# An adaLN transformer block on one core: out-projection ahead of the scores, down products in groups on alternate rows, the last layernorm in two parts

## Chip, core and metric

The kernel runs on 1 core of one Trainium2 chip. The metric is the device time of one execution in microseconds. Shown runs are compared by their medians.

## The reference

The kernel computes one block of a transformer for a batch of 2 sequences of 1024 rows and 256 columns, all in fp32. Cut to what matters:

```python
mod = (silu(c) @ wmod).reshape(B, 6, 1, 256)
sa, ca, ga, sb, cb, gb = ...                    # ga, gb: kept away from zero
h = layernorm(x) * (1 + ca) + sa
q, k, v = h @ Wq + bq, h @ Wk + bk, h @ Wv + bv # 16 heads of 128
q, k = rotary(q * 128 ** -0.5), rotary(k)
attn = softmax(causal(q @ k.T))                 # per head, 1024 x 1024
x = x + ga * ((attn @ v) @ Wo + bo)
h = layernorm(x) * (1 + cb) + sb
gate, up = qlinear(h, wq_gate, s_gate), qlinear(h, wq_up, s_up)   # 704 hidden units
x = x + gb * qlinear(silu(gate) * up, wq_down, s_down)
```

`qlinear` takes integer weights, less 128, times a scale for each output.

## The kernel before

**Units and slots.** The work of attention is cut into 32 units, one for each sequence and head (`units`, n from 0 to 31; two heads h form a group g that shares its loaded weights). A unit has 8 slots, one for each tile of 128 query rows. The order of all instructions is written out by hand (`tc.manual_schedule()`), so each engine's queue holds its instructions in the order of the program. The engines only wait for one another by semaphores.

**A slot.** In slot i, `score` (L410) multiplies 128 rows of q with the (i+1) x 128 keys that the causal mask leaves, into a tile of `ps_sc` (two buffers), and DVE finds the negative maximum of each row with one masked reduction (L425). `turned` (L452) transposes the exponentials of the slot before on DVE, in 32x32 blocks, into `t32` (L456). After every fourth slot, 16 transfers on SP's queue (L468) move these blocks into `pT`, which completes the transposition. `expo` (L437) makes the exponentials on ACT. Then `project_out` (L502) follows: one matmul `py` (L509) into the only buffer of `ps_y`, and a DVE instruction (L512) that scales by the row's softmax denominator and adds to x. It works on heads of earlier units: in slots 0 to 3 on the rows 512 to 1023 of unit n-2, in slots 4 to 7 on the rows 0 to 511 of unit n-1. After it `release` (L405) runs the part of the rotary product that had been put off, on DVE and POOL. Then come projections of the next unit's q, k (L379) and v (L361), in slots 5 and 6 the product of the previous unit's `pT` with v for its rows 512 to 1023 (`values`, L483, matmul `po`), and in slot 7 the same for the unit's own rows 0 to 511. `extras` spreads further work over the units, among it the layernorm of the second sequence for attention (units 10 to 14) and that of the first sequence for the gated part (units 26 to 30); both put instructions on DVE.

**The gated part.** The hidden layer has 704 units, that is `NF` = 6 chunks: five of 128 and a last one of 64 (`FULL` = 640). `hidden(b, blk, c)` (L525) computes gate and up of one chunk for 512 rows: 4 matmuls of 512 columns, silu on ACT and one product on DVE into `gTs`. The last chunk has gate and up in one matmul pair. In unit 31, slots 1 to 6 hold `hidden(0, 0, c)` with banks from `ps_a`, with `late=False`; the later ones use `ps_sc`. ACT needs one table for exponentials, one for silu and one for the root, and loads it anew at each change. `down(b, blk, j)` (L555) multiplies one tile of 128 rows with the six chunks of `wdT`, adds x on DVE (`yo`) and sends the tile to `out` on SP's queue. `bank` (L496) hands out four PSUM banks in turn: `ps_y`, `ps_o` and twice `ps_a`. The chunk 5 of `wdT` holds its 64 rows twice, in the partitions 0 to 63 and 64 to 127; before, only the first copy is read.

**The end.** After unit 31 come `hidden(0, 1, c)`, the rest of `project_out` and `values`, and the layernorm of the second sequence: `ln_stats` of 8 tiles, one `ln_sqrt` (ACT), `ln_scale` and `ln_turn` (transposes on PE, `ptx`, and a DVE instruction L217) for two blocks of four tiles. Between them stand `down(0, 0, j)`. Then `hidden(1, 0, c)` and `hidden(1, 1, c)` follow, with one `down` of the block before after each of the chunks 1 to 4, and four `down` at the very end.

Of the kernel before, what the change touches and what calls it, by code (L numbers as in the profile page):

```python
# [11 lines left out]
F32 = mybir.dt.float32  # L12
I32 = mybir.dt.int32
AF = mybir.ActivationFunctionType
ALU = mybir.AluOpType
PSUM = bass.MemoryType.PSUM

P = 128
B, S, D = 2, 1024, 256
H, DH = 16, 128  # L20
HID = 704
NT = S // P
# [15 lines left out]
def adaln_block(ctx: ExitStack, tc: tile.TileContext, a, cos_d, sin_d, out):  # L38
# [457 lines left out]
    def bank(name):  # L496

        pool, tag = banks[turn[0] % 4]
        turn[0] += 1
        return pool.tile([P, 512], F32, tag=tag, name=name)  # L500

    def project_out(u, t, late=False):  # L502

        b, g, h = u
        if t % 4 == 0:
            nc.vector.reciprocal(rdens[u][:, t : t + 4], dens[u][:, t : t + 4])
        name = f"py_{b}{g}{h}{t}"
        py = bank(name) if late else ps_y.tile([P, 512], F32, tag="y", name=name)
        nc.tensor.matmul(  # L509
            py[:, :D], outs[u][:, ts(t, P)], weights[b, g]["o"][:, h, :], start=True, stop=True  # L510
        )
        nc.vector.scalar_tensor_tensor(  # L512
            x[b][:, t, :], py[:, :D], rdens[u][:, t : t + 1], x[b][:, t, :], ALU.mult, ALU.add
        )
# [10 lines left out]
    def hidden(b, blk, c, late=True):  # L525
        if c == 0:
            gTs[b, blk] = fpool.tile([P, NF, QB], F32, tag="f", name=f"gT_{b}{blk}")
        last = c == NF - 1
        if late:
            pg = ps_sc.tile([P, S], F32, tag="sc", name=f"pgu_{b}{blk}{c}")  # L530
            pgs = [pg[:, ts(j, QB)] for j in range(2)]
        else:
            pgs = [
                ps_a.tile([P, 512], F32, tag="a", name=f"pgu_{b}{blk}{c}{j}") for j in range(2 - last)
            ]
        for pg, n in zip(pgs, ("gate",) if last else ("gate", "up")):
            for k in range(KC):
                nc.tensor.matmul(  # L538
                    pg,
                    wT["last"][:, k, :] if last else wT[n][:, k, ts(c, P)],  # L540
                    h2s[b, blk][:, k, :],
                    start=(k == 0),
                    stop=(k == KC - 1),
                )
        sg = ppool.tile([P, QB], F32, tag="p", name=f"sg_{b}{blk}{c}")
        if last:

            m = HID - FULL
            nc.scalar.activation(sg[m:], pgs[0][:m], AF.Silu)
            nc.vector.tensor_tensor(gTs[b, blk][:m, c, :], sg[m:], pgs[0][m:], ALU.mult)  # L550
        else:
            nc.scalar.activation(sg, pgs[0], AF.Silu)
            nc.vector.tensor_tensor(gTs[b, blk][:, c, :], sg, pgs[1], ALU.mult)

    def down(b, blk, j):  # L555
        t = blk * 4 + j
        pd = bank(f"pd_{b}{t}")
        for c in range(NF):
            m = min(P, HID - c * P)
            nc.tensor.matmul(  # L560
                pd[:, :D],
                gTs[b, blk][:m, c, ts(j, P)],
                wdT[b][:m, c, :],
                start=(c == 0),
                stop=(c == NF - 1),
            )
        yo = rot.tile([P, D], F32, tag="r1", name=f"yo_{b}{t}")
        nc.vector.tensor_tensor(yo, pd[:, :D], x[b][:, t, :], ALU.add)
        nc.sync.dma_start(out[b, ts(t, P), :], yo)


    units = [(b, g, h) for b in range(B) for g in range(NG) for h in range(HG)]
# [53 lines left out]
    with tc.manual_schedule():  # L626
        nc.scalar.activation(
            sc.rearrange("p b k -> p (b k)"), sc.rearrange("p b k -> p (b k)"), AF.Silu
        )
        nc.scalar.activation(warm, eps_t, AF.Sqrt)  # L630
        weights[0, 0] = {}
        load_w(0, 0, "q")
        load_w(0, 0, "k")
        for t, t_d in ((cos_t, cos_d), (sin_t, sin_d)):
            nc.sync.dma_start(t[:, :QB], t_d[:, :QB])
        load_w(0, 0, "v")
        for t in (4, 6):
            load_x(0, t, 2, nc.sync)
        for t, t_d in ((cos_t, cos_d), (sin_t, sin_d)):
            nc.sync.dma_start(t[:, QB:], t_d[:, QB:])  # L640
        nc.sync.dma_start(wga, a["w_gates"])
        nc.sync.dma_start(wmod[:, 1], a["L0_wmod"][1])
        load_proj(*units[2][:2])
        load_out(0, 0)
        nc.gpsimd.memset(bvacc, 0.0)

        for blk, t in enumerate(t32):
            for j in range(3):
                nc.gpsimd.memset(t[:, :, j, 4 * blk + j + 1 :, :], 0.0)
        for t in (0, 2):  # L650
            for j in range(2):
                ln_stats(0, "a", t + j)
            ln_sqrt(0, "a", t, t + 2)
            if t:
                ln_scale(0, "a", 0, (0, 1))
        modulation(0, ps_y, "y")
        ln_scale(0, "a", 0, (2, 3))
        shift_scale(0)
        ln_turn(0, "a", 0, 0, new_hT(0, 0), split=True)
        for t in range(4, NT):  # L660
            ln_stats(0, "a", t)
        ln_sqrt(0, "a", 4, NT)
        for s in ("q", "k"):
            project_qk(units[0], s, 0)
        for t in (0, 2):
            project_v(0, 0, t, *((ps_o, "o"), (ps_y, "y"))[t // 2])
        ln_scale(0, "a", 1)
        release()
        ln_turn(0, "a", 1, 0, new_hT(0, 1), split=True)
        gates()  # L670
        for s in ("q", "k"):
            project_qk(units[0], s, 1)
        nc.gpsimd.dma_start(bo_bc, a["L0_attn_bo"].to_broadcast([P, D]))

        for n, u in enumerate(units):
            b, g, h = u
            prev = units[n - 1] if n else None
            nxt = units[n + 1] if n + 1 < N else None
            nb, ng = (b, g + 1) if g + 1 < NG else (b + 1, 0)
            more = nb < B  # L680
            for i in range(NT):
                ps, nmax = score(u, i)
                if i >= 1:
                    turned(u, i - 1)
                elif prev:
                    turned(prev, NT - 1)
                expo(u, i, ps, nmax)

                if i < 4 and n > 1:
                    project_out(units[n - 2], 4 + i)  # L690
                if i >= 4 and prev:
                    project_out(prev, i - 4)
                release()
                if i in (1, 3, 4, 6) and nxt:
                    project_qk(nxt, *{1: ("q", 0), 3: ("k", 0), 4: ("q", 1), 6: ("k", 1)}[i])
                if i in (5, 6) and prev:
                    values(prev, 1, 4 * (i - 5), 4 * (i - 4))

                if i == 7 and prev:
                    values(u, 0, 0, 4)  # L700
                if n == 1 and i == 1:
                    values(prev, 0, 0, 4)
                if i in (0, 2):
                    if h == 0:
                        project_v(b, g, 4 + i)
                    elif more:
                        project_v(nb, ng, i)
                if not nxt and 1 <= i < 7:
                    hidden(0, 0, i - 1, late=False)
                extras(n, i)  # L710
                if i == 7 and h == 1:
                    if more:
                        load_out(nb, ng)
                    if n + 3 < N:
                        load_proj(*units[n + 3][:2])

        u, prev = units[-1], units[-2]
        turned(u, 7)
        for c in range(4):
            hidden(0, 1, c)  # L720
            project_out(prev, 4 + c, late=True)
            project_out(u, c, late=True)
        values(u, 1, 0, 8)
        hidden(0, 1, 4)
        for t in range(4, NT):
            project_out(u, t, late=True)
        hidden(0, 1, 5)
        for t in range(NT):
            ln_stats(1, "b", t)
        ln_sqrt(1, "b", 0, NT)  # L730
        down(0, 0, 0)
        ln_scale(1, "b", 0)
        down(0, 0, 1)
        down(0, 0, 2)
        ln_turn(1, "b", 0, 2, new_h2(1, 0))
        down(0, 0, 3)
        ln_scale(1, "b", 1)
        for c in range(NF):
            hidden(1, 0, c)
            if c == 0:  # L740
                ln_turn(1, "b", 1, 2, new_h2(1, 1))
            if c in (1, 2, 3, 4):
                down(0, 1, c - 1)
        for c in range(NF):
            hidden(1, 1, c)
            if c in (1, 2, 3, 4):
                down(1, 0, c - 1)
        for j in range(4):
            down(1, 1, j)


def _rotary_tables():
# [65 lines left out]
```

## Time and profile before

| | |
|---|---|
| time, median of 3 runs | 1099.24 us (1099.04 to 1101.0) |
| profiled execution: its own time | 1098.96 us |
| profiled execution: span | 1097.2 us |
| busy PE, DVE, ACT, POOL | 1085.3, 641.6, 508.4, 397.4 us |
| instructions | 12347 |

The profile comes from one execution; its span runs from the first to the last instruction that it shows, and lies 1.76 us under that execution's own time. PE is TensorE's matmuls, PEld its weight loads, DVE is VectorE, ACT ScalarE, POOL GpSimd, SP the SyncE, whose queue issues most transfers. A row of a timeline has the start, the duration, engine and line, the operation, the written and the read tiles and their shapes, how many instructions are merged in it, and in brackets how long the engine had stood idle before it and for whom. In a row of the waits, the engine and line that waited stand first, then for whom, then the time in total, the number of waits and the longest. Durations of matmuls include their filling and draining, which overlaps with the next one's; what one costs in a row of many is seen from start to start.

### The profile page before, as it was taken

Reading aid. Unit: us, or ns where it says so; the run is one execution under the profiler, and the core shown is the slowest. Engines: PE = TensorE matmul, PEld = TensorE weight load, DVE = VectorE, ACT = ScalarE, POOL = GpSimd, SP = SyncE. Lnnn points to the kernel's source line nnn. Section 1 sums busy time; section 2 is a strip of 40 time slices with the busy share of each in tenths; the row PEclk is TensorE's granted clock in tenths of the full one; section 3 lists DMA queues with packets and bytes.
Section 4 is the critical chain, followed back from the end, with each engine's and each line's share of the span. In section 5 each row is a group of like instructions: output and inputs, shape, how many; then the busy total and the mean of one; then the engine's idle time right before and its main releaser. Section 6 shows DMA issues by size and latency. Waiting matters only on the chain.

```text
span 1097.2 us, 12347 instructions
## 1 busy us (share of the span) xinstructions
PE 1085.3 (99%) x3524; PEld 641.0 (58%) x3524; DVE 641.6 (58%) x1418; ACT 508.4 (46%) x953; POOL 397.4 (36%) x364
## 2 busy tenths in 40 slices
PE   9999999999999999999999999999999999999998
PEld 5555555656565565655565666565655556455555
DVE  5556565666766855655566565556668656544311
ACT  5644444544555444444454454444445445641110
POOL 4635353535343343754333533333333334100000
PEclk9999999999999999999999999999999999999999
DMA  6365656657564556465554646464545656431000
GB/s 216 81 146 125 158 127 162 151 115 179 127 147 106 133 120 156 97 148 116 139 130 109 145 109 145 108 147 99 138 97 134 133 124 136 91 83 25 25 20 29
DMA packets 67192, 130.97 MB, mean 119 GB/s; under 512 B 18963, under 2 KB 23315, under 8 KB 67125
## 3 DMA queue, kind: packets, MB, share of 16 engines
q1 hardware_dynamic: 64772, 125.91, 48.6%
q10 hardware_dynamic: 2304, 4.16, 1.2%
q8 instruction: 28, 0.46, 0.2%
q14 instruction: 40, 0.32, 0.1%
q0 software_dynamic: 48, 0.13, 0.1%
HBM read 25.26 MB, written 2.10 MB: 25 GB/s over the span
## 4 chain that ended last, share of the span: by engine, by line
PE 96%; DVE 3%; issue 0%; ACT 0%; POOL 0%; DVEq 0%; ACTq 0%; POOLq 0%
PE ps L422 22%; PE po L483 22%; PE py L509 10%; PE pq L379 10%; PE pk L379 10%; PE pv L361 9%; PE pgu L538 7%; PE pd L560 4%; DVE t L456 1%; DVE ps L425 1%; PE warm_ps L82 1%; DVE x L512 0%; DVE kT L395 0%; PE pm L119 0%; PE pg L150 0%
## 5 line engine op out<-in xcount | busy, mean ns | idle before, releaser
L425 DVE CUSTOM_DVE_ANT_0 ps<-ps,mask 128x128 f32<-128x128 f32 (+7 forms) x256 | 195.6, 764 | 328.6 <-PE ps L422 328.2
L442 ACT ACTIVATE p<-ps,nmax 128x128 f32<-128x128 f32 (+7 forms) x256 | 189.8, 741 | 340.4 <-DVE nmax L425 336.9
L422 PE MATMUL ps<-kT,qT 128*128 128x512 f32 (+3 forms) x768 | 289.6, 486 | 0.7 <-ACT p L442 0.7
L483 PE MATMUL po<-pT,v 128*128 128x512 f32 (+3 forms) x768 | 263.4, 486 | 0.0
L422 PEld LDWEIGHTS ps<-kT,qT 128*128 128x128 f32 x768 | 141.1, 190 | 127.3 <-issue 121.0
L483 PEld LDWEIGHTS po<-pT,v 128*128 128x128 f32 x768 | 145.8, 190 | 115.6 <-issue 92.0
L456 DVE STREAM_TRANSPOSE t<-p 128x128 f32<-128x128 f32 (+7 forms) x256 | 198.2, 774 | 0.3
L509 PE MATMUL py<-wo,o 128*128 128x256 f32 x512 | 156.9, 390 | 5.0 <-DVE x L512 5.0
L392 POOL TENSOR_TENSOR r_k<-r_k,sin_t 128x512 f32<-128x512 f32 x64 | 81.3, 1271 | 208.5 <-ACT r_k L391 208.4
L398 POOL TENSOR_TENSOR kT<-kT,r_k 128x512 f32<-128x512 f32 x64 | 81.5, 1273 | 158.2 <-DVE kT L395 153.0
L392 POOL TENSOR_TENSOR r_q<-r_q,sin_t 128x512 f32<-128x512 f32 x64 | 81.8, 1278 | 148.9 <-ACT r_q L391 145.8
L509 PEld LDWEIGHTS py<-wo,o 128*128 128x128 f32 x512 | 90.0, 190 | 64.9 <-issue 30.1
L361 PE MATMUL pv<-wv,hT 128*128 128x256 f32 x512 | 120.9, 379 | 1.1 <-DVE qT L395 1.1
L379 PE MATMUL pq<-hT,wq 128*128 128x512 f32 x256 | 120.5, 593 | 0.5 <-DVE hT L217 0.5
L512 DVE SCALAR_TENSOR_TENSOR x<-py,rden,x 128x256 f32<-128x256 f32 x256 | 116.0, 455 | 7.5 <-PE py L509 0.7
L379 PE MATMUL pk<-hT,wk 128*128 128x512 f32 x256 | 120.3, 592 | 0.0
L391 ACT ACTIVATE r_q<-pq,cols 64x512 f32<-64x512 f32 x128 | 87.5, 683 | 47.9 <-PE pq L379 47.0
L361 PEld LDWEIGHTS pv<-wv,hT 128*128 128x128 f32 x512 | 97.1, 190 | 15.2 <-DVE qT L395 1.2
L391 ACT ACTIVATE r_k<-pk,cols 64x512 f32<-64x512 f32 x128 | 87.4, 683 | 18.0 <-PE pk L379 15.9
L398 POOL TENSOR_TENSOR qT<-qT,r_q 128x512 f32<-128x512 f32 x64 | 83.6, 1306 | 25.5 <-DVE qT L395 23.1
L379 PEld LDWEIGHTS pk<-hT,wk 128*128 128x128 f32 x256 | 48.6, 190 | 35.8 <-issue 32.0
L379 PEld LDWEIGHTS pq<-hT,wq 128*128 128x128 f32 x256 | 48.4, 190 | 35.3 <-issue 31.2
(87 smaller groups left out, 699.1 us busy)
## 6 DMA issues: line engine op xcount, KB each, us to landing
pT<-t SPq DMA_DIRECT2D x512, 128.0 KB, 2.4
pT<-t SPq DMA_DIRECT2D x512, 64.0 KB, 2.0
wq<-in_Wq SPq DMA_DIRECT2D x16, 256.0 KB, 3.1
wk<-in_Wk SPq DMA_DIRECT2D x16, 256.0 KB, 4.0
wv<-in_Wv SPq DMA_DIRECT2D x16, 256.0 KB, 4.2
wo<-in_Wo SPq DMA_DIRECT2D x16, 256.0 KB, 2.9
out<-yo SPq DMA_DIRECT2D x16, 128.0 KB, 1.7
x<-in_x SPq DMA_DIRECT2D x4, 256.0 KB, 5.2
```

What stands on the lines that cost most here:

```text
L361: nc.tensor.matmul(pv[:, ts(j, HG * DH)], hT[b, n][:, k, ts(r, P)], weights[b, g]["v"][:, k, :], start=(k == 0), stop=(k == KC - 1),)
L379: nc.tensor.matmul(pq, weights[b, g][s][:, k, ts(h, DH)], hT[b, n][:, k, :], start=(k == 0), stop=(k == KC - 1),)
L391: nc.scalar.activation(r1[to], pq[of], AF.Identity, bias=cols[of, c : c + 1])
L392: nc.gpsimd.tensor_tensor(r1, r1, sin_t[:, sl], ALU.mult)
L398: nc.gpsimd.tensor_tensor(dst[:, sl], dst[:, sl], r1, ALU.add)
L422: nc.tensor.matmul(ps[:, c:e], qT[:, ts(i, P)], kT[:, c:e], start=True, stop=True)
L425: nc.vector.tensor_tensor_reduce(ps[:, :L], ps[:, :L], mask[:, NT - 1 - i :, :].rearrange("p t k -> p (t k)"), -SCALE, FLT_MAX, ALU.add, A ...
L442: nc.scalar.activation(p[:, :L], ps[:, :L], AF.Exp, bias=nmax, scale=-1.0, accum_out=dens[u][:, i : i + 1])
L456: nc.vector.transpose(t32[blk][:, :, j, : i + 1, :].rearrange("p c k b -> p k c b"), p[:, : (i + 1) * P].rearrange("p (k c a) -> p k c a", ...
L483: nc.tensor.matmul(po[:, off * P :], vs[b, g][:, k, ts(h, DH)], pT[:, off:, :, k, :], start=(k == 0), stop=(k == last),)
L509: nc.tensor.matmul(py[:, :D], outs[u][:, ts(t, P)], weights[b, g]["o"][:, h, :], start=True, stop=True)
L512: nc.vector.scalar_tensor_tensor(x[b][:, t, :], py[:, :D], rdens[u][:, t : t + 1], x[b][:, t, :], ALU.mult, ALU.add)
```

## The change

Five edits:

- In a slot, `project_out` moves from behind `expo` to ahead of `score`. On PE, py then stands ahead of the score's matmuls; on DVE, the addition into x stands ahead of the slot's reduction and transpose.
- `hidden(0, 0, c)` moves from slots 1 to 6 of unit 31 to its slots 0 to 5.
- `down` takes two or four tiles. It first multiplies the five full chunks of each tile, and then the 64-row chunk of each, alternately from the partitions 0 to 63 and 64 to 127. For that, the last chunk's product in `hidden` is written in two halves: tiles 0 and 2 of the block to the lower partitions, 1 and 3 to the upper ones. The output tiles `yo` come from the pool `xn` with four buffers, but for the first block.
- The last layernorm works in two parts of four tiles, each with its own statistics, root and scaling. The first part begins ahead of the last `values`.
- The `down` calls are regrouped: two pairs for block (0, 0), a group of four for each of (0, 1) and (1, 0), after chunk 3 of the following `hidden`, and two pairs at the end.

```diff
             m = HID - FULL
             nc.scalar.activation(sg[m:], pgs[0][:m], AF.Silu)
-            nc.vector.tensor_tensor(gTs[b, blk][:m, c, :], sg[m:], pgs[0][m:], ALU.mult)
+            for j, rows_ in enumerate((slice(0, m), slice(m, P))):
+                part = lambda t: t.rearrange("p (t j q) -> p t j q", j=2, q=P)[:, :, j, :]
+                nc.vector.tensor_tensor(
+                    part(gTs[b, blk][rows_, c, :]), part(sg[m:]), part(pgs[0][m:]), ALU.mult
+                )
...
-    def down(b, blk, j):
-        t = blk * 4 + j
-        pd = bank(f"pd_{b}{t}")
-        for c in range(NF):
-            m = min(P, HID - c * P)
+    def down(b, blk, *js):
+        pds = {}
+        for j in js:
+            pds[j] = bank(f"pd_{b}{blk}{j}")
+            for c in range(NF - 1):
+                nc.tensor.matmul(
+                    pds[j][:, :D],
+                    gTs[b, blk][:, c, ts(j, P)],
+                    wdT[b][:, c, :],
+                    start=(c == 0),
+                    stop=False,
+                )
+        for j in js:
+            half = ts(j % 2, HID - FULL)
             nc.tensor.matmul(
-                pd[:, :D],
-                gTs[b, blk][:m, c, ts(j, P)],
-                wdT[b][:m, c, :],
-                start=(c == 0),
-                stop=(c == NF - 1),
+                pds[j][:, :D],
+                gTs[b, blk][half, NF - 1, ts(j, P)],
+                wdT[b][half, NF - 1, :],
+                start=False,
+                stop=True,
             )
-        yo = rot.tile([P, D], F32, tag="r1", name=f"yo_{b}{t}")
-        nc.vector.tensor_tensor(yo, pd[:, :D], x[b][:, t, :], ALU.add)
-        nc.sync.dma_start(out[b, ts(t, P), :], yo)
+        for j in js:
+            t = blk * 4 + j
+            if (b, blk) == (0, 0):
+                yo = rot.tile([P, D], F32, tag="r1", name=f"yo_{b}{t}")
+            else:
+                yo = xnp.tile([P, D], F32, tag="xn", name=f"yo_{b}{t}")
+            nc.vector.tensor_tensor(yo, pds[j][:, :D], x[b][:, t, :], ALU.add)
+            nc.sync.dma_start(out[b, ts(t, P), :], yo)
...
             for i in range(NT):
+                if i < 4 and n > 1:
+                    project_out(units[n - 2], 4 + i)
+                if i >= 4 and prev:
+                    project_out(prev, i - 4)
                 ps, nmax = score(u, i)
...
                 expo(u, i, ps, nmax)
-
-                if i < 4 and n > 1:
-                    project_out(units[n - 2], 4 + i)
-                if i >= 4 and prev:
-                    project_out(prev, i - 4)
                 release()
...
-                if not nxt and 1 <= i < 7:
-                    hidden(0, 0, i - 1, late=False)
+                if not nxt and i < NF:
+                    hidden(0, 0, i, late=False)
...
+        for t in range(4):
+            ln_stats(1, "b", t)
+        ln_sqrt(1, "b", 0, 4)
         values(u, 1, 0, 8)
+        ln_scale(1, "b", 0)
         hidden(0, 1, 4)
         for t in range(4, NT):
             project_out(u, t, late=True)
         hidden(0, 1, 5)
-        for t in range(NT):
+        ln_turn(1, "b", 0, 2, new_h2(1, 0))
+        for t in range(4, NT):
             ln_stats(1, "b", t)
-        ln_sqrt(1, "b", 0, NT)
-        down(0, 0, 0)
-        ln_scale(1, "b", 0)
-        down(0, 0, 1)
-        down(0, 0, 2)
-        ln_turn(1, "b", 0, 2, new_h2(1, 0))
-        down(0, 0, 3)
+        ln_sqrt(1, "b", 4, NT)
+        down(0, 0, 0, 1)
         ln_scale(1, "b", 1)
+        down(0, 0, 2, 3)
+        ln_turn(1, "b", 1, 2, new_h2(1, 1))
         for c in range(NF):
             hidden(1, 0, c)
-            if c == 0:
-                ln_turn(1, "b", 1, 2, new_h2(1, 1))
-            if c in (1, 2, 3, 4):
-                down(0, 1, c - 1)
+            if c == 3:
+                down(0, 1, 0, 1, 2, 3)
         for c in range(NF):
             hidden(1, 1, c)
-            if c in (1, 2, 3, 4):
-                down(1, 0, c - 1)
-        for j in range(4):
-            down(1, 1, j)
+            if c == 3:
+                down(1, 0, 0, 1, 2, 3)
+        down(1, 1, 0, 1)
+        down(1, 1, 2, 3)
```

## The prediction

> **What bounds the kernel now.** The first section of the page came first: PE is busy nearly all of the span and no other engine comes near it.
>
> ```profile
> PE 1085.3 (99%) x3524; PEld 641.0 (58%) x3524; DVE 641.6 (58%) x1418; ACT 508.4 (46%) x953; POOL 397.4 (36%) x364
> ```
>
> The granted clock is 9 in all forty slices, so only two things shorten this kernel: gaps between matmuls, or less PE work. I therefore laid the start of each PE record against the next. Without a wait a 512-column record takes 0.429 us, one of 256 columns 0.216, one of 128 columns 0.109, and each matmul of the program makes two records. What exceeds this sums to 28.6 us: 13.7 in front of or inside the out-projection py, 6.1 around the 64-row records of pd, 0.6 at the last layernorm's transposes, and 8 before or near the first unit, which the change doesn't touch. The waits say who holds py back.
>
> ```profile
> PEld py L509 <- DVE x L512: 12.4, 30, 1.9
> ...
> PE py L509 <- DVE x L512: 5.0, 5, 1.5
> ```
>
> Third, the timeline of one unit boundary (unit 2 begins at 75.75), PE alone and then DVE alone:
>
> ```profile
> 73.16 0.59 PE L509 MATMUL py<-wo,o 128*128 128x256 f32 x2
> 73.59 2.32 PE L483 MATMUL po<-pT,v 128*128 128x512 f32 x8
> 75.75 0.39 PE L422 MATMUL ps<-kT,qT 128*128 128x128 f32 x2
> 76.04 0.70 PE L509 MATMUL py<-wo,o 128*128 128x256 f32 x2
> 76.57 1.89 PE L361 MATMUL pv<-wv,hT 128*128 128x256 f32 x8
> 78.30 0.59 PE L422 MATMUL ps<-kT,qT 128*128 128x256 f32 x2
> 78.73 0.68 PE L509 MATMUL py<-wo,o 128*128 128x256 f32 x2
> ```
>
> ```profile
> 73.36 1.23 DVE L425 CUSTOM_DVE_ANT_0 ps<-ps,mask 128x1024 f32<-128x1024 f32 x1 [3.67 <-PE ps L422]
> ...
> 74.51 1.11 DVE L456 STREAM_TRANSPOSE t<-p 128x896 f32<-128x896 f32 x1
> 75.54 0.44 DVE L512 SCALAR_TENSOR_TENSOR x<-py,rden,x 128x256 f32<-128x256 f32 x1
> 75.90 0.74 DVE L395 SCALAR_TENSOR_TENSOR kT<-pk,cols,cos_t 128x512 f32<-128x512 f32 x1
> 76.56 0.29 DVE L425 CUSTOM_DVE_ANT_0 ps<-ps,mask 128x128 f32<-128x128 f32 x1
> ...
> 76.76 1.24 DVE L456 STREAM_TRANSPOSE t<-p 128x1024 f32<-128x1024 f32 x1
> ```
>
> The py of slot 7 is done at 73.6, but its addition into x starts at 75.54, behind the 1024-wide reduction and a transpose. The single y bank is free at 75.98, so slot 0's py starts at 76.04 instead of 75.97, and costs 0.10 more because its weights could not be loaded ahead.
>
> **1. py ahead of the score: what it removes.** An ordinary boundary loses 0.174 at slot 0 and 0.078 at slot 1; units 11, 12, 27, 28 and 31 lose 0.79, 1.82, 0.79, 1.82 and 1.98, where layernorm work on DVE (or, in 31, nothing else on PE in slot 0) lies between. 25 x 0.252 + 7.2 = 13.5. With py first, the addition runs while PE does the score, before the reduction can start, and the bank is free long before the next py. Three places keep something. In units 12 and 28 DVE still owes 1.6 us of layernorm (L228, L198, L201, from 372.37 to 373.93 in unit 12) ahead of slot 0's addition; put after one another from score 7's end, DVE's rows have that addition end at 374.72, while PE, which starts unit 12 at 371.56, wants slot 1's py 2.38 later, at 373.94: with the unhidden weight load 0.94 each. In unit 31 gate and up move to slot 0 and cover the 1.98; but now the addition stands between one product of gate and up and the next reduction, so the loop on DVE and ACT of product, addition, reduction, table load 1.28, exponential, table load 1.28 and silu grows by 0.36, and its first turn takes 5.6 where PE's slot 1 takes 4.3: gate of slot 2, which wants the bank that silu empties, waits about 0.6. Kept: 2.5. Gain 11.0.
>
> **2. What it delays.** Score 7 now ends 0.43 later within its slot (one py), and so does its reduction. At slot 0 the DVE queue then holds reciprocal and addition of py ahead of the reduction and the transpose of row tile 7, where it had only slot 7's addition. From the rows: reduction 73.79, transpose 74.94, kT 75.97, reciprocal 76.63, addition 76.87, reduction 77.23, transpose 77.44 instead of 76.76: 0.67 later. Behind that transpose stand 16 transfers of pT on SP's queue, issued one at a time:
>
> ```profile
> 78.07 10.03 SPq L468 DMA_DIRECT2D pT<-t  x16
> ...
> 166.63 11.03 SPq L468 DMA_DIRECT2D pT<-t  x16
> ```
>
> The last issue of the first round begins 0.59 before its end, at 87.5, and lands 2.4 later, at 89.9; PE's first po on it starts at 91.72. That spare time of 1.8 us shrinks by 0.67 and by the 0.25 that PE no longer loses: by 0.92. From the one round that already touched (unit 10, spare 0.31, a 0.07 delay) PE waits once less than 0.38 is left. Ordinary units keep 0.5. But ten rounds issue or land late: spare 1.06, 0.49, 0.53, 0.76, 0.31, 0.75, 0.79, 1.03, 0.54, 1.05. Each waits 1.30 less its spare, together 5.6 with unit 28's 0.54 counted so. Units 11, 12, 27 and 28 also lose more of their old stalls, which adds 0.05, 0.47, 0.2 and 0.6. Cost 6.9; bounds 0 (a late round may recover) and 10. Other rounds (first four tiles) have 2.1, at least 0.9, and lose 0.43: nothing.
>
> **3. Down products.** The weight loads of the last group show the 64-row chunk.
>
> ```profile
> 1084.30 0.29 PEld L560 LDWEIGHTS pd<-wdT,gT 64*128 64x128 f32 x2 [0.33 <-issue]
> 1084.93 2.02 PEld L560 LDWEIGHTS pd<-wdT,gT 128*128 128x128 f32 x10 [0.33 <-issue]
> 1087.28 0.29 PEld L560 LDWEIGHTS pd<-wdT,gT 64*128 64x128 f32 x2 [0.33 <-issue]
> ```
>
> A tile takes 2.98 us, where twelve records of 0.216 make 2.59: going to 64 rows and back costs 0.39. Sixteen tiles become six groups: 10 x 0.39 = 3.9 saved. Inside a group the 64-row products alternate between upper and lower rows, which no row here shows. Bounds: a change of half that costs as much as a change of height (10 x 0.2 = 2.0 lost), and full overlap of eight pairs (8 x 0.43 = 3.5 saved). I take the overlap of a tile's second record with the next tile's first, since two records on the same rows follow one another here: one record in a pair, three in a group of four, (4 + 6) x 0.216 = 2.1 saved. The Trainium skill (TensorEngine Tiling, Theoretical Speedup) gives up to 2x for two row tiles; by that the saving would be the 3.5, and the sum 1.4 lower. No row here shows it.
>
> **4. Last layernorm in two parts.** One more root on ACT, so two more table loads, 1.28 each. The first lies beside values (5.6 us). The second delays silu of gate/up 4: load at 1.9 after values end, silu until 3.8, product until 4.5, four additions until 6.4; the transposes want their banks at 6.9: hidden, by 0.5. Today transposes and pd lose 0.6 there. Afterwards the second block's transposes follow directly on two down tiles whose banks they need: wait 0.4. Gain 0.2.
>
> **5. Small things.** Halving the last product costs DVE 0.16 four times, beside PE work. The last two tiles' additions end on one another: 0.2 at the end. The bursts of four additions (1.7) precede gate/up 4, which lasts 3.4: hidden. The new output buffers and gate/up without products between (banks come free 1.0 after their matmuls, asked for 3.4 later): nothing.
>
> **Sum.** -11.0 + 6.9 - 3.9 - 2.1 - 0.2 + 0.2 = -10.1. The profiled execution took 1098.96 (span 1097.2), 0.28 below the median, so 1088.9, or 1089 as a median.
>
> **Rivals.** *No new wait.* The late rounds come from other traffic and instruction loads on the queues and may fall elsewhere; then term 2 is zero: 1082. Against: units 14, 19 and 23 are among the ten and have no other load beside them, and the loads beside the others stay. *No overlap of halves*: 1091. *Slower.* The transfers of pT become the bound in all 28 units. That decides when the transpose of tile 7 comes later than forecast by over 0.5; each further us costs 28. Equal to today at 0.7 more, and at 1.0 more (28, less the 9 that 18 ordinary units still hold) 1108. For: all rounds hang on one DVE queue, which this change lengthens at just that place. Against: every step of that queue is a row above, and DVE is idle before 73.36. *A dearer table change.* If ACT also had to empty at each change, for as long again as the load's own 1.28, silu 4 and the additions would pass the transposes' 6.9 by some 0.5 with the reload: 1089.5. Against: silu of unit 31 ends at 949.16 and the load of the next table starts at 949.18; another silu starts 1.29 after its load. The Trainium skill (ScalarE: Activation LUTs, What ACT_TABLE_LOAD costs) adds a drain of about 1380 ns to the 1283 of a load; the trace shows the 1283 and no such drain.
>
> **Numbers.** Forecast 0.50, no new wait 0.25, no overlap 0.17, slower 0.05, dearer tables 0.03. The range takes in the first two rivals and, above, waits of 10 with half the overlap: 1081.5 to 1094. About 0.2%, 2.2 us, is what a measurement can tell from no change. All cases but one lie over that below: faster 0.94; same 0.01, slower 0.05.
>
> **What would show it.** Right: no wait of py on x L512 outside units 12, 28 (and few tenths elsewhere); a few waits of po on pT, each under 1.4, in units with late rounds; two 64-row changes per group, tiles of a pair ending closer than 0.43. Wrong: po waiting in ordinary units (term 2 too small), no po wait at all (too large), four 64-row products lasting 8 x 0.216 (no overlap), or a gap before the transposes of block 0.

## The result, and the profile after

The changed kernel takes 1085.63 us (median of 4 runs, 1085.48 to 1086.76), the kernel before beside it 1099.32 (4 runs): the ratio is 0.9875, with a 95% interval of 0.9857 to 0.9892. Two later sets of runs of the changed kernel gave medians of 1085.72 and 1086.44. The forecast was 1089. The profiled execution took 1085.72 us with a span of 1083.9, which is 13.3 less than before's span.

The first section of the page: PE is busy for 13.3 us less on the same 3524 records, so no work was removed: what went is time between the starts of records, in which they waited, or followed one another where they now overlap. The page counts much of it as busy, because a record's drawn length covers it.

```profile
PE 1072.0 (99%) x3524; PEld 638.7 (59%) x3524; DVE 655.5 (60%) x1422; ACT 507.6 (47%) x956; POOL 397.2 (37%) x364
```

The waits (engine and line that waited, for whom: total, times, longest). Where py waited 30 times it waits 4 times; what is new is po waiting for pT.

```profile
PEld py L509 <- DVE x L512: 3.3, 4, 1.1
PEld po L483 <- DMA pT<-t: 2.9, 4, 1.1
...
PE po L483 <- DMA pT<-t: 1.6, 3, 0.8
...
PE py L509 <- DVE x L512: 1.4, 2, 0.7
```

The timeline of the unit boundary that was shown of before (unit 2 now begins at 76.09), PE and then DVE:

```profile
71.78 0.60 PE L509 MATMUL py<-wo,o 128*128 128x256 f32 x2
72.21 1.88 PE L422 MATMUL ps<-kT,qT 128*128 128x512 f32 x4
73.93 2.32 PE L483 MATMUL po<-pT,v 128*128 128x512 f32 x8
76.09 0.60 PE L509 MATMUL py<-wo,o 128*128 128x256 f32 x2
76.52 0.38 PE L422 MATMUL ps<-kT,qT 128*128 128x128 f32 x2
76.74 1.89 PE L361 MATMUL pv<-wv,hT 128*128 128x256 f32 x8
78.47 0.59 PE L509 MATMUL py<-wo,o 128*128 128x256 f32 x2
```

```profile
76.31 0.71 DVE L395 SCALAR_TENSOR_TENSOR kT<-pk,cols,cos_t 128x512 f32<-128x512 f32 x1
76.94 0.16 DVE L506 RECIPROCAL rden<-den 128x4 f32<-128x4 f32 x1
77.21 0.48 DVE L512 SCALAR_TENSOR_TENSOR x<-py,rden,x 128x256 f32<-128x256 f32 x1
77.61 0.29 DVE L425 CUSTOM_DVE_ANT_0 ps<-ps,mask 128x128 f32<-128x128 f32 x1
77.81 0.14 DVE L425 DVE_READ_ACCUMULATOR2_ANT nmax<- 128x1 f32 x1
77.81 1.24 DVE L456 STREAM_TRANSPOSE t<-p 128x1024 f32<-128x1024 f32 x1
```

From py to py PE now runs without a gap: 76.09, 0.43 later the score, 0.22 later pv, 1.73 later the next py. The price stands in the DVE rows: the transpose of row tile 7 waits behind the reciprocal, the addition and the reduction. It starts 1.72 after the unit's begin on PE, where it was 1.01 before (76.76 less 75.75).

The rounds of 16 transfers on SP's queue (start, duration) begin 3.03 after the unit's begin instead of 2.32. The second one shown is one with a late issue, as in before:

```profile
79.12 10.02 SPq L468 DMA_DIRECT2D pT<-t  x16
...
166.94 10.93 SPq L468 DMA_DIRECT2D pT<-t  x16
```

The weight loads of the 64-row chunk (here the first pairs, block (0, 0)): four loads come at once, and the change of height is paid once for two tiles.

```profile
1005.07 0.30 PEld L575 LDWEIGHTS pd<-wdT,gT 64*128 64x128 f32 x4 [0.33 <-issue]
1005.70 4.18 PEld L566 LDWEIGHTS pd<-wdT,gT 128*128 128x128 f32 x20 [0.33 <-issue]
1010.22 0.30 PEld L575 LDWEIGHTS pd<-wdT,gT 64*128 64x128 f32 x4 [0.33 <-issue]
```

Last, the place where the change lost something, the transposes of the last layernorm on PE and, below, ACT ahead of the first of them:

```profile
999.73 1.09 PE L210 MATMUL ptx_b<-ident,xn_b 128*128 128x128 f32 x8 [0.76 <-DVE x L512]
...
1011.43 1.09 PE L210 MATMUL ptx_b<-ident,xn_b 128*128 128x128 f32 x8 [0.51 <-DVE yo L588]
```

```profile
995.61 1.28 ACT L557 ACT_TABLE_LOAD   x1 [2.89 <-PE pgu L538]
996.90 0.60 ACT L557 ACTIVATE sg<-pgu 128x512 f32<-128x512 f32 x1
```

What the starts of PE's records exceed their streaming time by fell from 28.6 to 14.8 us. By place, counted in the same way as for the prediction:

| place | forecast | measured | from |
|---|---|---|---|
| py, with gate in unit 31 | -11.0 | -10.95 | 13.71 to 2.20, and 0.56 at gate of slot 2 |
| po waiting for pT | +6.9 | +3.3 | 0.07 to 3.40 |
| 64-row chunk: changes of height | -3.9 | -3.9 | sixteen to six |
| 64-row chunk: overlap | -2.1 | -3.4 | 8 pairs of 0.43 |
| last layernorm | -0.2 | +1.0 | 0.68 to 1.71 |
| end, from the last record's start | +0.2 | +0.45 | 3.63 to 4.07 |
| start of the kernel | 0 | +0.3 | differs from run to run |

### The profile page after: what moved, and what is told of

It reads as the page before. It is cut to its first block, busy times and chain, and to the rows that moved or that the text cites. A ratio compares the mean times of both kernels' runs of the same rounds, so it can differ in the third digit from the quotient of the medians.

```text
span 1083.9 us, 12352 instructions
## 1 busy us (share of the span) xinstructions
PE 1072.0 (99%) x3524; PEld 638.7 (59%) x3524; DVE 655.5 (60%) x1422; ACT 507.6 (47%) x956; POOL 397.2 (37%) x364
## 4 chain that ended last, share of the span: by engine, by line
PE 95%; DVE 2%; SPq 1%; DMA 1%; ACT 1%; issue 0%; DVEq 0%; ACTq 0%
PE po L483 23%; PE ps L422 22%; PE pk L379 10%; PE pq L379 10%; PE py L509 10%; PE pv L361 10%; PE pgu L538 6%; PE pd L566 3%; SPq L468 1%; DMA pT<-t 1%; DMA wmod<-in_wmod 0%; PE pd L575 0%; ACT L557 0%; DVE ps L425 0%; DVE t L456 0%
## 5 line engine op out<-in xcount | busy, mean ns | idle before, releaser
L512 DVE SCALAR_TENSOR_TENSOR x<-py,rden,x 128x256 f32<-128x256 f32 x256 | 123.0, 482 | 182.9 <-PE py L509 176.2
L422 PEld LDWEIGHTS ps<-kT,qT 128*128 128x128 f32 x768 | 145.7, 190 | 77.5 <-issue 62.9
L509 PE MATMUL py<-wo,o 128*128 128x256 f32 x512 | 151.5, 380 | 1.4 <-DVE x L512 1.4
L509 PEld LDWEIGHTS py<-wo,o 128*128 128x128 f32 x512 | 92.3, 190 | 67.3 <-issue 51.2
L361 PEld LDWEIGHTS pv<-wv,hT 128*128 128x128 f32 x512 | 94.9, 190 | 19.9 <-DVE qT L395 1.2
L398 POOL TENSOR_TENSOR qT<-qT,r_q 128x512 f32<-128x512 f32 x64 | 83.6, 1306 | 31.1 <-DVE qT L395 28.6
L379 PEld LDWEIGHTS pq<-hT,wq 128*128 128x128 f32 x256 | 46.1, 190 | 33.8 <-issue 31.2
```

Of the source, the lines that this page charges most:

```text
L361: nc.tensor.matmul(pv[:, ts(j, HG * DH)], hT[b, n][:, k, ts(r, P)], weights[b, g]["v"][:, k, :], start=(k == 0), stop=(k == KC - 1),)
L379: nc.tensor.matmul(pq, weights[b, g][s][:, k, ts(h, DH)], hT[b, n][:, k, :], start=(k == 0), stop=(k == KC - 1),)
L398: nc.gpsimd.tensor_tensor(dst[:, sl], dst[:, sl], r1, ALU.add)
L422: nc.tensor.matmul(ps[:, c:e], qT[:, ts(i, P)], kT[:, c:e], start=True, stop=True)
L509: nc.tensor.matmul(py[:, :D], outs[u][:, ts(t, P)], weights[b, g]["o"][:, h, :], start=True, stop=True)
L512: nc.vector.scalar_tensor_tensor(x[b][:, t, :], py[:, :D], rdens[u][:, t : t + 1], x[b][:, t, :], ALU.mult, ALU.add)
```

## The experiments

In the first four, two parts of the change and two suspected costs were tried, beside the kernel before, whose median was 1100.22 there. That is 0.9 more than beside the result, while the times expected of these four start from 1085.6 or 1099.3; a difference of this size from an expected time says nothing. The next four are the changed kernel (1085.72) and three runs beside it, and so are the last four (1086.44).

**py ahead of the score, alone.** The kernel before with this edit only:

```diff
             for i in range(NT):
+                if i < 4 and n > 1:
+                    project_out(units[n - 2], 4 + i)
+                if i >= 4 and prev:
+                    project_out(prev, i - 4)
                 ps, nmax = score(u, i)
...
                 expo(u, i, ps, nmax)
-
-                if i < 4 and n > 1:
-                    project_out(units[n - 2], 4 + i)
-                if i >= 4 and prev:
-                    project_out(prev, i - 4)
                 release()
```

> The kernel before, with project_out ahead of the score as the only change. Theory (from the two traces): the waits of py go from 13.7 us to about 3.2 (0.95 each in units 12 and 28, about 1.0 in unit 31, whose slot 0 still has no gate and up), and po waits on late rounds of pT for about 3.4: 1099.3 - 10.5 + 3.4 = 1092. Rival 1, no cost at po: 1089. Rival 2, the forecast's 6.9 at po: 1096. In the trace the spare time between a round's landing and po should be near 0.87 us in ordinary units where it was 1.8.

Measured: 1093.58, ratio 0.9936 (0.9914 to 0.9958). This is 1.6 above the 1092 expected; as a gain on the kernel before it is 6.6 for 7.3. In its trace py costs 3.4 and po 6.2. Of these 6.2, 3.8 come from a single place, unit 14, in a way that nothing of the prediction held: po waited 2.05 us there, and the records after it ran at half speed. The execution of this trace took 1095.35, 1.8 over the median, so the half speed need not have been in the others.

```profile
446.37 5.37 PE L483 MATMUL po<-pT,v 128*128 128x512 f32 x8 [1.89 <-DMA pT<-t]
```

Eight records of 512 columns take 3.6 us elsewhere; these take 5.4. The granted clock fell to 0.5 at 446.60 for 3.41 us. Without this place po costs 2.4. So the part that was meant to gain gains, and gives back a part at pT.

**All but that.** The changed kernel with `project_out` behind `expo`, as before:

> The changed kernel with project_out back behind expo; all else as changed. Theory: py waits 11.7 us again (all of before but unit 31, which gate and up in slot 0 cover), gate of unit 31 no longer waits its 0.56, and po waits nothing: 1085.6 + 11.7 - 2.2 - 0.6 - 3.4 = 1091. If the new place earned nothing, 1085.6; if the new order costs nothing at po, 1094.5.

Measured: 1092.66, ratio 0.9939 (0.9916 to 0.9961), 1.7 above what was expected; as a gain it is 7.6 for 8.3. Its profiled execution took 1097.51, 4.9 over the median. In it the granted clock was 0.5 from 8.55 to 15.38, near the start, and po waits 2.5 us in unit 14, here at a clock of 1.0 all through. py costs 11.9 in it, and an ordinary round again has 1.8 us to spare, against 0.87 in the changed kernel. The two parts alone gain 6.6 and 7.6 us, together 14.2; the whole change gained 13.7 beside its own runs of before. They add up to within 0.5.

**64-row products on the lower rows only.** Groups as in the change, but no alternation:

```diff
-            half = ts(j % 2, HID - FULL)
+            half = slice(0, HID - FULL)
```

with the last chunk's product written in one piece to the lower partitions.

> The changed kernel, but all 64-row products of down read the lower 64 partitions, so no two of them can share the array; the groups of two and four stay. Theory: the overlap of halves is worth 3.4 us (eight products of 0.43), the fewer changes of height stay: 1085.6 + 3.4 - 0.3 (the last two additions no longer end on one another) = 1088.7. As the forecast put it (only one record of a pair and three of a group overlap, 2.1): 1087.4. If overlap were worth nothing: 1085.6.

Measured: 1088.01, between the 1088.7 and the 1087.4 expected, so the time does not decide between them; the records do. The four 64-row records of a pair on PE, first here, then in the changed kernel:

```profile
1005.87 1.13 PE L571 MATMUL pd<-wdT,gT 64*128 64x256 f32 x4
...
1006.93 4.58 PE L562 MATMUL pd<-wdT,gT 128*128 128x256 f32 x20
```

```profile
1005.07 0.70 PE L575 MATMUL pd<-wdT,gT 64*128 64x256 f32 x4
1005.71 4.58 PE L566 MATMUL pd<-wdT,gT 128*128 128x256 f32 x20
```

From start to start 1.06 us against 0.64: alternation takes away 0.42 for each pair, two whole records of 0.216. Over the eight pairs the trace has 3.42, for a forecast of 2.1.

**The rest of kT behind the transpose.** The changed kernel with the postponed rotary product of k (the 0.63 of kT on DVE in the rows above) put behind the transpose of row tile 7:

```diff
                 expo(u, i, ps, nmax)
-                release()
+                if i < 7:
+                    release()
```

> The changed kernel, with the DVE step of kT (line 395 of slot 7) put off until slot 0, behind the transpose of row tile 7. If DVE's queue ahead of that transpose sets when the pT rounds start, they start 0.5 us earlier, the spare time in ordinary units goes from 0.87 to 1.35 and the waits of po from 3.4 us to about 0.7: 1083 unless the bank of k, which is now freed 0.65 later, makes slot 1's projection of q wait (up to 0.1 a unit, then 1085). If the rounds start late for another reason (SP's own queue), the spare time stays 0.87 and the time 1085.6.

Measured: 1086.95, ratio 0.988 (0.9856 to 0.9904): none of the three times expected, and no gain. The rounds did win 0.5 of spare time (0.87 to 1.4), and the waits of po fell, but for unit 14, to 1.1 us. Unit 14 has a wait of 2.07 and the half speed again, in an execution that took 3.3 over the median. In their place the projection of q in slot 1 now waits for ACT (v, L368), some 0.1 in each unit and 2.5 in all, and up in unit 31 waits 0.8 for kT. What was won at one place was given back at the next.

**The changed kernel again**, beside the following three:

> The changed kernel once more, as the control of the runs beside it on this chip. All theories expect its former 1085.6, within 1, and its po waits between 2 and 4 us, the late rounds in other units than before if the lateness of a single DMA issue is chance, in the same units if it belongs to the program.

Measured: 1085.72. po waits 3.98 us. The issues after which the next one starts over 0.85 us later, where 0.63 is usual, fall into the same 19 rounds as in the first trace: the lateness is no chance, but belongs to the program.

**The silu table early.** At the end of the kernel:

```diff
         ln_sqrt(1, "b", 0, 4)
+        nc.scalar.activation(warm, ones[:, :1], AF.Silu)
         values(u, 1, 0, 8)
...
-        ln_turn(1, "b", 1, 2, new_h2(1, 1))
         for c in range(NF):
             hidden(1, 0, c)
+            if c == 0:
+                ln_turn(1, "b", 1, 2, new_h2(1, 1))
```

> The changed kernel with a one-column silu on ACT directly behind the first root, so that the silu table is loaded while PE does the last values, and with the turning of the second block of the last layernorm put behind the first chunk's hidden instead of ahead of it. Theory (silu of chunk 4 waits for gate and up of the whole tile, and its table load stands between it and the four additions that the transposes wait for): the waits of 0.93 ahead of the first block's transposes and of 0.58 and 0.10 ahead of the second block's vanish, 1.5 less than the changed kernel beside it. Rival (the transposes wait for banks that down holds, whatever ACT does): only the second vanishes, 0.6 less.

Measured: 1084.57, so 1.15 less. The load now stands directly behind the root, and the transposes follow without a wait (ACT, then PE):

```profile
991.18 1.28 ACT L747 ACT_TABLE_LOAD   x1
...
996.54 0.60 ACT L557 ACTIVATE sg<-pgu 128x512 f32<-128x512 f32 x1 [2.91 <-PE pgu L538]
```

```profile
998.01 1.88 PE L538 MATMUL pgu<-h,wlastT 128*128 128x512 f32 x4
999.73 1.04 PE L210 MATMUL ptx_b<-ident,xn_b 128*128 128x128 f32 x8
```

Both waits at the transposes are gone from the trace (1.71 to 0), and gate and up give 0.2 of it back; that makes the 1.5 expected, and the medians show somewhat less. The rival, that banks held by down are what counts for the first block, falls.

**The last layernorm in one part.** Statistics of eight tiles, one root, two scalings, as before the change; the rest as changed:

```diff
-        for t in range(4):
-            ln_stats(1, "b", t)
-        ln_sqrt(1, "b", 0, 4)
         values(u, 1, 0, 8)
-        ln_scale(1, "b", 0)
...
-        ln_turn(1, "b", 0, 2, new_h2(1, 0))
-        for t in range(4, NT):
+        for t in range(NT):
             ln_stats(1, "b", t)
-        ln_sqrt(1, "b", 4, NT)
+        ln_sqrt(1, "b", 0, NT)
         down(0, 0, 0, 1)
-        ln_scale(1, "b", 1)
+        ln_scale(1, "b", 0)
         down(0, 0, 2, 3)
-        ln_turn(1, "b", 1, 2, new_h2(1, 1))
+        ln_turn(1, "b", 0, 2, new_h2(1, 0))
+        ln_scale(1, "b", 1)
         for c in range(NF):
             hidden(1, 0, c)
+            if c == 0:
+                ln_turn(1, "b", 1, 2, new_h2(1, 1))
```

> The changed kernel with the last layernorm in one part, as before the change (eight statistics, one root, then the pair of downs, scaling, the second pair, the turnings), but with down in groups and all the rest as changed. Theory (the split earns nothing as it lies: it removed 0.68 of waits and brought 1.6): the same as the changed kernel within 0.5, or up to 1 less. Rival (the split hides a chain of statistics, root and scaling that would otherwise stand ahead of the transposes): 1.5 to 3 more.

Measured: 1085.97 beside 1085.72. In the traces the transposes wait 0.73 instead of 1.71, and gate and up exceed their streaming time by 1.80 instead of 1.00, so the end is as long in both. As it lies in the changed kernel, the split earns nothing.

**One microsecond more on DVE.** Two statistics instructions on the mask, ahead of slot 0's transpose of row tile 7, in every unit:

```diff
+                    for w_ in (4, 2):
+                        more_st = small.tile([P, 6], F32, tag="st", name=f"more_{n}_{w_}")
+                        nc.vector.bn_stats(more_st, mask[:, :w_, :].rearrange("p t k -> p (t k)"))
                     turned(prev, NT - 1)
```

> The changed kernel with two more statistics instructions on DVE, about 1.05 us together, ahead of slot 0's transpose of tile 7 in every unit; their results are not used. Theory (the rounds of pT transfers have 0.87 us to spare in an ordinary unit, and what DVE delays beyond 0.5 is waited for by po): ordinary units wait about 0.55 each and units with a late issue up to 1.05 more, together 17 to 22 more, 1103 to 1107. Rival (the transfers of pT are not what po waits for, or their round can be caught up): the same within 1.

Measured: 1101.29, so 15.6 more, and 1.9 over the kernel before (ratio 1.0016, 1.0006 to 1.0025). DVE, then PE in the same unit:

```profile
78.19 1.01 DVE L713 BATCH_NORM_STATS2 more<-mask 128x6 f32<-128x512 f32 x2
79.12 1.23 DVE L456 STREAM_TRANSPOSE t<-p 128x1024 f32<-128x1024 f32 x1
```

```profile
92.58 2.81 PE L483 MATMUL po<-pT,v 128*128 128x512 f32 x6 [0.23 <-DMA pT<-t]
```

The transpose came 0.93 later, not 1.05, so an ordinary round that had 0.87 to spare is 0.06 short; with the 0.38 below which PE waits this makes 0.44. The trace has 0.47 in this unit and 0.2 to 0.6 in the other ordinary ones. po costs 18.2 instead of 4.0, py 4.0 instead of 2.2, which is the whole difference. The forecast of 17 to 22 was a little high: it counted 1.05 where the transpose moved by 0.93. This is the place where the rival "slower" of the prediction sits: 0.9 us of further delay on DVE takes the whole gain away.

**The changed kernel a third time**, beside the last three:

> The changed kernel as the control of this chip. All theories: 1085.6 within 1.

Measured: 1086.44; po waits 4.7 us. Fifteen of the 19 rounds have a late issue again; for the other four the round next to each has it, and one more is new.

**PE's instructions shifted by 128.** Why single issues on SP's queue are late was open. The page also lists transfers under the name instruction; by this name and their count they are taken here for loads of an engine's own instructions. In the trace of the changed kernel each of the 16 transfers of 16 KB on the queue that the page calls q8 instruction that begin within a round of pT has an issue of over 0.85 us beside it. One such transfer comes for every 256 instructions of PE. So the count was shifted:

```diff
-    for n in range(3):
-        warm_up(4)
+    for n in range(35):
+        nc.tensor.matmul(warm_ps[:, :4], ones, ones[:, :4], start=True, stop=True)
```

> The changed kernel with 128 more instructions at the head of PE's queue: three warm-up matmuls of 512 columns give way to 35 of four columns (results not used), so that PE reaches every later instruction with 128 more behind it. In the traces so far one transfer of 16 KB on the DMA queue that the page names instruction (q8) starts for every 256 instructions of PE, within 50 of them, and nearly every one that falls into a round of pT transfers has one issue on SP's queue beside it that takes 0.9 to 2.0 instead of 0.59. Theory (the load holds up the issue): with the loads shifted by half their distance the late rounds move. Rounds at the start of units 5, 9, 10, 14 and 28, late so far, are in time in at least three of the five; of those at the start of units 2, 3, 7, 16, 17, 21, 26 and 30, in time so far, at least four have an issue of over 0.85; nearly each load within a round has its late issue. Rival (an issue is late by its place in SP's queue or by what it moves): the same rounds as before are late. The total of po's waits stays between 2 and 5 by both; the time is up to 8 more, by the slower warm-up at the start, which is not the point.

Measured: 1099.99 in the one execution, 13.6 more than the changed kernel beside it where at most 8 were expected; the last section says where they lie. The rounds at the starts of units 21 and 28, in the changed kernel and then here (start, duration of the 16 issues on SP's queue):

```profile
638.79 10.04 SPq L468 DMA_DIRECT2D pT<-t  x16
...
845.47 11.08 SPq L468 DMA_DIRECT2D pT<-t  x16
```

```profile
652.98 11.16 SPq L468 DMA_DIRECT2D pT<-t  x16
...
860.74 10.03 SPq L468 DMA_DIRECT2D pT<-t  x16
```

The late one is in time and the timely one late. Of the five rounds named as late so far, all have their issues in time, though unit 14's still lands late; of the eight named as in time, three are late (units 7, 21 and 26), one fewer than expected; the other late ones are rounds of the first four tiles. All 14 loads that fall into a round have a late issue beside them. The only rounds that are late in both are four whose late issue, here of 0.9 to 1.0, stands at a fixed place of SP's own queue (its 335th, 463rd and 591st instruction, and the 1103rd). po waits 4.0 in all. So a late issue moves with the loads of PE's instructions, and a round into which one falls is late. In the fourteen traces of this study 220 of 224 loads of this kind within a round had a late issue, which takes 1.4 to 1.6 on average instead of 0.63. Why the issue has to wait for the load the traces do not show.

**Layernorm steps off the boundary.** The steps of the layernorms that DVE did in slot 7 of units 11 and 27 and in slot 0 of the next ones are done in slots 1 to 4 of these next ones:

```diff
-            t = 8 * (n - m + 3) + i - 2
+            t = {m - 3: i - 2, m - 2: i + 4}.get(n, -1) if 1 <= i <= (6 if n == m - 3 else 4) else -1
```

> The changed kernel with the steps of the layernorms in units 11 and 27 taken out of slot 7 and of slot 0 of the next unit and done in slots 1 to 4 of units 12 and 28 instead. Theory (these steps on DVE hold the addition of units 12 and 28 and with it py by 0.94 each, and the rounds of pT of these two units): both waits of py vanish, 1.9, and the waits of po in units 12 and 28, 0.7 and 1.0, fall to at most 0.6 together, in all 2.5 to 3.2 less. Rival (the steps only move to where the rest of DVE's queue waits for them): less than 1 gained.

Measured: 1083.67, so 2.8 less than the changed kernel beside it. py falls from 2.19 to 0.31 in the trace, and the waits of po in units 12 and 28 are all but gone (0.5 and 0.95 in the trace beside it, here 0.1 at most). What the prediction booked as kept in these two units was indeed these steps.

**The best version.** This edit, that of the silu table, and one more: in slot 0 the transpose of row tile 7 stands between the addition and the reduction.

```diff
+                if i == 0 and prev:
+                    turned(prev, NT - 1)
                 ps, nmax = score(u, i)
                 if i >= 1:
                     turned(u, i - 1)
-                elif prev:
-                    turned(prev, NT - 1)
```

> The changed kernel with three edits: the early silu table and the later turning of the end, the layernorm steps off the boundary, and in slot 0 the transpose of row tile 7 ahead of the slot's reduction on DVE instead of behind it. Theory: 1.2 for the first (as measured), 2.5 to 3.2 for the second, and for the third the rounds of pT start 0.2 to 0.3 earlier, so that each of the some six late rounds waits 0.2 less, 1.2: together 5 less, 1080 to 1081.5. Rival for the third (the reduction of slot 0, now 1.2 later, holds up the exponentials and by them the scores of slot 2): 0 to 10 lost.

Measured: 1080.64 (1080.15 to 1081.81), ratio to the kernel before 0.9832 (0.9818 to 0.9845), where the changed kernel beside it had 0.9879 (0.9865 to 0.9892): 5.8 us less, inside the 1080 to 1081.5 expected. No run has the third edit alone; less the 1.15 and 2.8 of the other two, 1.9 are left for it, and part of that can be late rounds that fell elsewhere. DVE at the boundary of unit 2:

```profile
77.38 0.48 DVE L512 SCALAR_TENSOR_TENSOR x<-py,rden,x 128x256 f32<-128x256 f32 x1
77.78 1.23 DVE L456 STREAM_TRANSPOSE t<-p 128x1024 f32<-128x1024 f32 x1
78.94 0.27 DVE L425 CUSTOM_DVE_ANT_0 ps<-ps,mask 128x128 f32<-128x128 f32 x1
```

Ordinary rounds have 1.08 to spare instead of 0.87, and po's waits fall from 4.7 to 0.6 us. The rival of the third edit has a trace only in unit 31, where gate of two slots waits, 0.56 and 0.74, instead of one 0.46 (each without the 0.10 of a weight load that could not go ahead).

## Why the prediction was right, and where it was not

The sign held, and so did the mechanisms of the largest terms; the time lies inside the range, 3.4 below the forecast. It was too slow by 3.6 at the waits of po and by 1.3 at the overlap, and too fast by 1.2 at the last layernorm, by 0.25 at the end and by 0.3 at the start; that these offset one another in part is luck. Step by step:

**Term 1, py ahead of the score, -11.0: right, to the parts.** Units 12 and 28 keep 0.94 each, as worked out (0.84 and the unhidden weight load of 0.10), and gate of slot 2 in unit 31 waits 0.56 (0.46 and again 0.10) where about 0.6 stood. The run with the moved steps shows that the 0.94 came from the rows that were named.

**Term 2, what it delays, +6.9: mechanism right, size wrong.** The shift was right: spare time of an ordinary round fell from 1.80 to 0.87, by 0.93 for a forecast of 0.92. Ordinary rounds do not wait, and the added microsecond shows that they begin to where it was said. The step that failed was "ten rounds issue or land late", taken over from the trace of before as if the same rounds had to be late again. In the changed kernel only four of these ten are late by over 0.7 (those at the starts of units 5, 9, 14 and 28), and several late issues fall into rounds of the first four tiles, which have 1.65 to spare and hardly wait. The run with the shifted count shows why: a round is late where a load of PE's instructions falls into it, and which one that is depends on the place of PE's instructions in their order, which the change itself alters. Unit 14's round is the exception (see the end). The rival *no new wait* had this ("instruction loads on the queues and may fall elsewhere") and was argued down with "the loads beside the others stay". What was measured, 3.3 to 4.6 in three traces, lies between it and the forecast.

**Term 3, down: half right.** The changes of height saved 3.9 as said. The overlap saved 3.4 for 2.1. The step that failed was "I take the overlap of a tile's second record with the next tile's first": the records of the two tiles do not follow one another tile by tile. In the trace the first records of both tiles of a pair start 7 ns apart, at 1005.072 and 1005.079, and so do the second ones, at 1005.392 and 1005.399. So the upper bound holds, which is also what the Trainium skill gives (TensorEngine Tiling (Array Packing), Theoretical Speedup: up to 2x for two row tiles): the trace agrees, with 0.42 of 0.43 saved for each pair. A rule was here nearer than my nearest row, which showed two records on the same rows and so could not speak of two different ones.

**Term 4, last layernorm, -0.2: wrong sign, by 1.2.** "Load at 1.9 after values end" was the failing number: the load came 3.7 after them (995.61 against 991.93). The silu waits for gate and up of the whole tile of `ps_sc`, not for gate alone. That was to be read from before's trace: there the silu of such a tile starts at 992.94, behind up (991.02 for 1.88). In unit 31, where gate and up have tiles of their own, the load starts at 942.06, directly behind gate (940.10 for 1.88) and ahead of up's end. Product, additions and the transposes' banks came later by as much, and the "hidden, by 0.5" became a wait of 0.93. The second block's 0.4 became 0.68. The run with the early table shows the mechanism, and that the repair is one instruction on ACT. The rival *dearer table change* gave the right place for the wrong reason: the load itself takes its 1.28.

**Term 5, small things, +0.2: too small by 0.25.** With full overlap both last tiles end together, so that two additions and two transfers follow one another after the last record.

## What to carry to other kernels

When an edit moves work across a queue, follow the step that it delays to the transfers behind it and write down their spare time; that number (0.87 us here) said more about the next edits than the gain did. Rounds that are late in one trace need a cause before they are carried into a forecast: if it moves with the program, count how many are late, not which. A table load is hidden only if the instruction ahead of it on its engine ends early enough, so look up what that instruction really waits for, the whole tile or the half that it reads.

## What the hardware showed that was not expected

- Two 64-row matmuls on different halves of the rows run fully side by side: 7 ns between their starts, and 1.06 us for eight records of 256 columns in a group of four (1034.83 to 1035.89), the change of height included.
- Loads of PE's instructions, 28 in the kernel, each hold up one DMA issue on SP's queue by some 0.8 us where they fall into a round.
- In two runs (py ahead of the score alone, and the rest of kT behind the transpose) a wait of PE of 2.05 and 2.07 us in unit 14 was followed by a granted clock of 0.5 for 3.41 us, which cost 1.8 more. A wait of 1.94 in the run with the slower DVE passed without that, and so did one of 2.5 in unit 14 in the run with `project_out` behind `expo`; the length of the wait alone does not decide. The Trainium skill (TensorE: Matmul & The Clock Gate, Part 1) gives a free-running window of 3413 ns and slows an idle PE after at least one such window. The length agrees with the trace; but the waits ahead of both falls were shorter than one window, and here the measurement decides.
- 35 warm-up matmuls of four columns, 15 us long, left the granted clock at 0.5 until 25.9. With three of 512 columns it was 1.0 from between 4.1 and 6.7 on, though in one trace (`project_out` behind `expo`) it was back at 0.5 from 8.55 to 15.38. The 13.6 us that the run lost are not all the clock's: the first product behind the warm-up starts at 16.08 instead of 5.68 in the trace beside it, and only some 3.6 more are lost until the first score (37.89 against 23.93).
- Still open: the round at the start of unit 14 lands late in every trace, by 0.5 to 4.0 us against the median round of its trace. In the shifted run all its issues are in time, but each transfer takes 4.3 to 4.6 us from issue to landing, where 2.4 is usual. Why they are slow at this place is not shown.
